# Weights of the convolution's second product: from channel-interleaved to one run of 128 per channel

## The chip, the cores and the metric

One core of a Trainium2 chip runs the whole program. The metric is the device time of one execution in microseconds; a lower time is better. Of the kernel before there are three timed runs and one profiled execution.

## What is computed

The input r has 8 sequences of 2048 steps and 512 channels. The reference normalises it over the channels, convolves each channel with its own long kernel (a state-space model with 64 complex states), applies gelu, normalises, and adds the input; then comes a gated recurrence-like block and a second residual. Cut to what matters here:

```
x = r
K = dplr_kernel(B, C, P, Q, Lam, step, 2048)          # one kernel of 2048 taps for each of 512 channels
h1 = irfft(rfft(layernorm(x)) * rfft(K))[:, :2048]    # causal convolution along the sequence
x = x + layernorm(gelu(h1 + D * layernorm(x), approximate=False))
x = x + layernorm(ffn(layernorm(x)))
```

The kernel computes the causal convolution without a Fourier transform. The sequence is cut into NJ = 16 blocks of P = 128 steps. Within a block a 128x128 matrix made of the first 128 taps is applied; what comes from all earlier blocks is carried by a state x of 128 numbers (64 complex states), which a chain of matrix products moves from block to block. A second product turns the state into output: for each channel a 128x128 matrix, which this text calls the channel's readout weights. All products are made in float16 halves, high and low, so that each product is three matmuls.

## The kernel before, in words

**Stages.** Up to about 150 us the kernel sets up: it reads the input block by block for the layer norm (`stats`, L585 on), builds the powers of the state matrix (`aps`), and runs the state chain for the first two groups of channels. From 158.5 to 656 us it convolves: 512 channels in NG = 16 groups of G = 32. Then the feed-forward part runs until 2899 us; its matmuls are those of L950.

**One group of the convolution** (g = 1 to 14) is a loop of 16 steps. In step s_ the kernel does `conv_mm` for two channels of group g, and between them a link of the chain of group g + 1: `chain_hi` (2 matmuls, L661) and `chain_lo` (1 matmul, L667, and then `split`, which writes the high half with ScalarE, L101, and the low half with VectorE, L102). The low half of a link is an operand of the next `chain_lo`. One `tap_step` and one `chain_in` (3 matmuls) follow. So TensorE has in a step 12 matmuls of `conv_mm`, 6 of the chain and in steps 1 to 12 three of a tap step. Beside it VectorE, ScalarE and GpSimd normalise the input of group g + 2 (`norm_x`: L641 GpSimd, L643 VectorE, L645 ScalarE, L647 GpSimd) and prepare the weights of the feed-forward part (L392 to L409). Group 0 has no chain beside it, and group 15 (`conv_last`) works in two passes, over 4 blocks and then over 12.

**The order.** In the groups the order on TensorE, VectorE, ScalarE and GpSimd is the order in which the program is written (`manual_schedule`), with each engine strictly in its own order. In the setup the order is chosen by a scheduler that plans with estimated durations. DMAs are all issued by SyncE's queue, in order.

**The readout weights** live in a tile `m` for each half group of HS = 16 channels: [128 partitions, 2 halves, 128 columns, 16 channels] before the change. The first 4 of the 128 columns are copied by GpSimd (`load_taps`, L683) from a tile `mb`; `tap_step` doubles the columns: it multiplies columns k to k + kw, for all 16 channels at once, with a power of the state matrix (3 matmuls of kw * 16 = 64, 128, 256 or 512 columns), and `split` writes the product to columns n + k to n + k + kw. There are 6 tap steps for each half group. `conv_mm` (L708) and `conv_last` (L744) then use one channel of `m` as the weights of three matmuls: a load of 128 columns that lie 16 elements apart. The other operand of the convolution, the first 128 taps, is in a tile `t0` (shown as `t`), laid out in the same interleaved manner, and is read by the three matmuls before.

`mm3` (L450 to L452) is the helper that issues three matmuls; the profile gives its lines, and the tile tells which product it is: pyt<-u,t and pyt<-x,m are the two halves of the convolution, pmt<-m,aps is a tap step, pxt<-u,bm is `chain_in`.

Of the kernel before, what the change touches and what calls it, by code (L numbers as in the profile page):

```python
# [10 lines left out]
F16 = mybir.dt.float16  # L11
# [8 lines left out]
P = 128  # L20
L = 2048
H = 512
NB = 8
# [5 lines left out]
HS = 16  # L29
# [30 lines left out]
def s4_gated_block(ctx, tc, a, dbg=None):  # L60
    nc = tc.nc
    V, S, T, Q = nc.vector, nc.scalar, nc.tensor, nc.gpsimd
# [33 lines left out]
    aps = kp.tile([P, LEV + 1, 2, P], F16, name="aps")  # L96
# [3 lines left out]
    def split(hi, lo, src):  # L100
        S.activation(hi, src, AF.Copy)  # L101
        V.tensor_tensor(lo, src, hi, ALU.subtract)  # L102
# [5 lines left out]
    cb = kctx.enter_context(tc.tile_pool(name="cb", bufs=2))  # L108
# [339 lines left out]
    def mm3(out, w, x, start=True, stop=True):  # L448

        T.matmul(out, lhsT=w(0), rhs=x(0), start=start, stop=False)  # L450
        T.matmul(out, lhsT=w(1), rhs=x(0), start=False, stop=False)
        T.matmul(out, lhsT=w(0), rhs=x(1), start=False, stop=stop)  # L452
# [28 lines left out]
    def forms(q, t, i, xa, pt):  # L481

        for h in range(2):
            for k in range(KT):
                T.transpose(pt[h][:, k], xa[h][:, k * P : (k + 1) * P], ident)  # L485
        b1 = FJ.tile([P, 2, 2, P], F32, name="b1", tag="un")
        ts = FJ.tile([P, 4, 2, P], F32, name="ts", tag="ws")
        for h in range(2):
            S.activation(b1[:, h], pt[h][:, 0:2], AF.Copy)
        V.tensor_tensor(ts[:, 0:2], pt[1].rearrange("p (a k) c -> p a k c", a=2), b1, ALU.subtract)  # L490
        V.tensor_tensor(ts[:, 2], pt[1][:, 2:4], ts[:, 0], ALU.subtract)
        V.tensor_tensor(ts[:, 3], ts[:, 2], pt[0][:, 2:4], ALU.subtract)

        def halves():
            if i == 0:
                xfs[q, t] = (FT if t % 2 else FE).tile([P, 7, 2, 2, BP], F16, name="xf")
            xf, cs = xfs[q, t], slice(i * P, (i + 1) * P)
            for f, src in ((slice(0, 3, 2), pt[0].rearrange("p (a k) c -> p a k c", a=2)), (1, pt[1][:, 2:4]), (slice(3, 7), ts)):
                split(xf[:, f, 0, :, cs], xf[:, f, 1, :, cs], src)

        return halves
# [15 lines left out]
    def early_y(sl, y):  # L517

        v = y.rearrange("p (c b) h -> p c b h", b=NB)
        for i in range(2):  # L520
            Q.tensor_copy(early["y"][i][:, :, sl], v[:, i:QC:2, 0:2])
# [58 lines left out]
    with ExitStack() as cctx:  # L580
# [93 lines left out]
        def load_taps(g):  # L674

            for sl in (2 * g, 2 * g + 1):
                t0 = cb.tile([P, 2, P, HS], F16, name="t0", bufs=3)
                base = kpad[:, sl, 1 : P + 1, :]
                tap = bass.AP(base.tensor, base.offset, [[HS, P], [2 * P * H, 2], [1, P * HS]])
                dma(out=t0.rearrange("p i t h -> p i (t h)"), in_=tap)  # L680
                t0s[sl] = t0
                m = cb.tile([P, 2, P, HS], F16, name="m", bufs=4)
                Q.tensor_copy(m[:, :, 0:4, :], mb[:, :, :, sl * HS : (sl + 1) * HS])  # L683
                ms[sl] = m

        def tap_step(sl, lv, k):
            m, n = ms[sl], 1 << lv
            kw = min(n, 512 // HS)
            pmt = pm_.tile([P, 512], F32, name="pmt")
            pv = pmt[:, 0 : kw * HS]  # L690
            mm3(pv, lambda i: aps[:, lv, i, :], lambda i: m[:, i, k : k + kw, :].rearrange("p k h -> p (k h)"))
            split(m[:, 0, n + k : n + k + kw, :].rearrange("p k h -> p (k h)"),
                  m[:, 1, n + k : n + k + kw, :].rearrange("p k h -> p (k h)"), pv)

        def tap_steps(g):
            steps = [(lv, k) for lv in range(2, LEV) for k in range(0, 1 << lv, min(1 << lv, 512 // HS))]
# [2 lines left out]
        def conv_mm(g, hg):  # L699

            u, x = us[g], xs_[g]
            if hg % 4 == 0:
                pys[g] = py.tile([P, 4, NJ * NB], F32, name="pyt")
            sl, hm = 2 * g + hg // HS, hg % HS
            t0, m = t0s[sl], ms[sl]
            o = pys[g][:, hg % 4, :]
            mm3(o, lambda i: t0[:, i, :, hm], lambda i: u[:, :, i, hg, :], stop=False)
            mm3(o[:, NB:], lambda i: m[:, i, :, hm], lambda i: x[:, :, i, hg * NB : (hg + 1) * NB], start=False)  # L708

        def conv_out(g, c4):  # L710

# [15 lines left out]
        def conv_last(g):  # L727

            u, x = us[g], xs_[g]
            yt = {}  # L730
            for j0, j1, hn in ((0, JF, HS), (JF, NJ, 4)):
                n = j1 - j0
                for sl in (2 * g, 2 * g + 1):
                    t0, m = t0s[sl], ms[sl]
                    if j0 == 0:
                        yt[sl] = cb.tile([P, NJ * NB, HS], F32, name="y")
                    y = yt[sl][:, j0 * NB : j1 * NB]
                    for h0 in range(0, HS, hn):
                        pyt = py.tile([P, hn, n * NB], F32, name="pyt")
                        for hm in range(h0, h0 + hn):  # L740
                            hg = sl % 2 * HS + hm
                            o, c = pyt[:, hm - h0], NB if j0 == 0 else 0
                            mm3(o, lambda i: t0[:, i, :, hm], lambda i: u[:, j0:j1, i, hg, :], stop=False)
                            mm3(o[:, c:], lambda i: m[:, i, :, hm],  # L744
                                lambda i: x[:, max(j0 - 1, 0) : j1 - 1, i, hg * NB : (hg + 1) * NB], start=False)
                        S.activation(y[:, :, h0 : h0 + hn], pyt.rearrange("p h c -> p c h"), AF.Gelu, scale=unsc)  # L746
                    if j0 == 0:
                        early_y(sl, yt[sl])
                    dma(out=y_d[j0:j1, :, sl].rearrange("j p b h -> p j (b h)"), in_=y.rearrange("p (j b) h -> p j (b h)", b=NB))
                if j0 == 0:  # L750
                    early_row(0, (1,))

            for i in range(2):
                pt = [pm_.tile([P, KT, P], F32, name="pmt") for _ in range(2)]
                forms(0, 0, i, [normed[i], normed[i + 2]], pt)()
            early_row(1)
            for cj in range(QC):
                dma(out=x1_d[cj, :, 0], in_=early[cj][1][:, 0])

        mb = cm.tile([P, 2, 4, H], F16, name="mb")  # L760
        for k in range(4):
            pmt = pm_.tile([P, 512], F32, name="pmt")
            lv, src = ((0, None), (0, 0), (1, 0), (1, 1))[k]
# [10 lines left out]
        for g in range(2):  # L774
            load_taps(g)
            for st_ in tap_steps(g):
                tap_step(*st_)
# [23 lines left out]
        for g in range(NG):  # L801
# [17 lines left out]
            with tc.manual_schedule(engines=MAN if nxt else MAN | {mybir.EngineType.SP}):  # L819
                if ahead:  # L820
                    load_taps(g + 1)
                    if g == NG - 2:
                        mctx.close()
                    taps = tap_steps(g + 1)
                    chain_in(g + 1, 0)
                if nn:
                    load_x(g + 2)
                if not nxt:
                    early_tiles()
                    for sl in (2 * g - 2, 2 * g - 1):  # L830
                        early_y(sl, ys[sl])
                    dma(out=fcol, in_=a["fcol"])
                    weights(2)
                    early_row(0, (0,))
                    conv_last(g)
                    continue
                norms = [(k - lag, part) for k in range(NJ // JP + 1) for part, lag in ((0, 0), (2, 1), (1, 0), (3, 1))]
                for s_ in range(NJ):
                    if s_ % 2 == 0 and s_:
                        conv_out(g, s_ // 2 - 1)  # L840
                    if nn:

                        d = ND1 if g == 1 else 0
                        while norms and s_ >= d and (s_ == NJ - 1 or len(norms) > 4 + 2 * NJ * (NJ - 1 - s_) // (NJ - d)):
                            norm_x(g + 2, *norms.pop(0))

                    conv_mm(g, 2 * s_)
                    if ahead and s_ < NJ - 1:
                        chain_hi(g + 1, s_)
                    conv_mm(g, 2 * s_ + 1)  # L850
                    if ahead and s_ < NJ - 1:
                        chain_lo(g + 1, s_)
                    if ahead and 1 <= s_ <= 12:
                        tap_step(*taps[s_ - 1])
                    if ahead and s_ < NJ - 2:
                        chain_in(g + 1, s_ + 1)
                    for f in work.get((g, s_), ()):
                        f()
# [395 lines left out]
    with tc.manual_schedule(engines=MAN | {mybir.EngineType.SP}):  # L1254
        before = None
        for n, (q, t) in enumerate(steps):
# [8 lines left out]
            for sl, key in enumerate(zs + gs if n else gs[:5] + zs + gs[5:]):  # L1265
                p = 16 * n + 2 * sl
# [85 lines left out]
```

## Time and profile before

| what | value |
|---|---|
| three timed runs | 2898.7, 2899.93, 2905.06 us; median 2899.93 |
| the profiled execution: its own time, its span | 2900.85 us, 2899.1 us |
| mean granted TensorE clock | 0.962 |
| busy: PE, weight loads, DVE, ACT, POOL | 89%, 78%, 73%, 51%, 41% |
| first and last matmul with weights from `m` | 158.5 and 655.6 us |
| matmuls pyt<-x,m (and as many pyt<-u,t) | 3 x 544 |
| DMA, mean over the span | 156 GB/s |

PE is the row of matmuls and PEld that of weight loads, which overlap matmuls. [...] Windows of a stage show in this order: the stretch, its length, the busy time of PE, PEld, DVE, ACT and POOL with the number of instructions, the granted clock, the share of DMA and its GB/s.

### The profile page before, as it was taken

How to read it: one execution, taken by the hardware profiler on the slowest of the kernel's cores; microseconds unless marked ns; L12 is line 12 of the kernel's file. 1: busy time of each engine (PE TensorE's matmuls, PEld its weight loads, DVE VectorE, ACT ScalarE, POOL GpSimd, SP SyncE). 2: the span in 40 equal slices, each digit the busy share in tenths (PEclk: the TensorE clock that was granted, in tenths of full speed). 3: DMA queues.
4: the chain of work that ended last, by engine and by line, in shares of the span. 5: the costliest groups of instructions: out<-in, count | busy, mean ns of one | idle time of the engine just before them, and what ended most of it. 6: DMA issues, size and time to landing. Idle time of an engine off the chain costs nothing.

```text
span 2899.1 us, 60027 instructions
## 1 busy us (share of the span) xinstructions
PE 2588.2 (89%) x23940; PEld 2255.6 (78%) x23940; DVE 2102.1 (73%) x4248; ACT 1478.8 (51%) x3091; POOL 1185.9 (41%) x1496
## 2 busy tenths in 40 slices
PE   4678888885999999999999998999999899999990
PEld 3367777774888888878888886888888788888870
DVE  7868877747666776667777776777777677777757
ACT  8956666643434443445555454454545445444435
POOL 5757667714112221114454341345443324443227
PEclk8789999987999999999999999999999999999995
DMA  6867878787423433324664443355554334532338
GB/s 233 304 209 241 259 251 260 241 248 189 154 66 95 114 84 96 91 88 124 160 172 135 121 124 99 101 159 167 145 149 120 117 89 147 151 117 89 95 119 298
DMA packets 521937, 451.10 MB, mean 156 GB/s; under 512 B 289974, under 2 KB 401080, under 8 KB 516664
## 3 DMA queue, kind: packets, MB, share of 16 engines
q1 hardware_dynamic: 521224, 446.74, 52.0%
q8 instruction: 187, 3.06, 0.4%
q14 instruction: 94, 0.77, 0.1%
q10 hardware_dynamic: 432, 0.52, 0.1%
HBM read 295.41 MB, written 151.78 MB: 154 GB/s over the span
## 4 chain that ended last, share of the span: by engine, by line
PE 50%; DVE 13%; ACT 5%; DMA 4%; issue 2%; POOL 1%; SPq 0%; POOLq 0%; DVEq 0%; ACTq 0%
PE u L950 47%; PE pt L485 1%; DVE u L992 1%; DMA z_d<-zc 1%; DVE cf L1051 1%; ACT xf L101 1%; DVE cd L1037 1%; DMA y<-y_d 1%; ACT gate L1016 1%; DVE sty L462 1%; DVE gate L1036 1%; ACT y L903 1%; DMA z_d<-zt 1%; DVE u2p L989 1%; DVE sth L462 1%
## 5 line engine op out<-in xcount | busy, mean ns | idle before, releaser
L950 PEld LDWEIGHTS <-w 128*128 128x128 f16 x15120 | 1482.0, 98 | 216.0 <-issue 30.8
L950 PE MATMUL u<-xf,w 128*128 128x256 f16 x8064 | 945.4, 274 | 32.1 <-ACT zt L1003 15.4
L950 PE MATMUL u<-cf,w 128*128 128x256 f16 x7056 | 825.9, 273 | 1.5 <-DVE cf L1051 1.5
L950 PE MATMUL u<-w,xf 128*128 128x256 f16 x2688 | 314.2, 275 | 15.2 <-DVE u L992 5.2
L1141 POOL TENSOR_TENSOR x1r<-x1r,zr 128x512 f32<-128x512 f32 x96 | 133.6, 1392 | 453.8 <-ACT zr L1140 344.6
L988 ACT ACTIVATE u2p<-u 128x256 f32<-128x256 f32 x256 | 96.7, 378 | 433.9 <-PE u L950 433.7
L1016 ACT ACTIVATE gate<-u,bias 128x512 f32<-128x512 f32 (+1 forms) x384 | 200.6, 574 | 217.9 <-PE u L950 217.8
L904 POOL TENSOR_TENSOR xr<-y,xr 128x512 f32<-128x512 f32 x120 | 160.1, 1354 | 351.7 <-ACT y L903 351.5
L950 PEld LDWEIGHTS <-xf 128*128 128x128 f16 x2688 | 264.6, 99 | 49.8 <-issue 10.7
L989 DVE TENSOR_TENSOR u2p<-u2p,u 128x256 f32<-128x256 f32 x256 | 106.8, 417 | 258.7 <-ACT u2p L988 256.8
L992 DVE TENSOR_TENSOR u<-u,u2p 128x512 f32<-128x512 f32 x256 | 179.0, 699 | 8.8
L647 POOL TENSOR_TENSOR u<-xg,u 128x512 f16<-128x512 f32 x104 | 128.7, 1242 | 124.6 <-ACT u L645 124.6
L641 POOL TENSOR_TENSOR xg<-xg,mu 128x512 f32<-128x512 f32 x112 | 162.7, 1459 | 9.7 <-DMA xg<-in_xr 9.7
L471 POOL TENSOR_TENSOR rsy<-rsy,nhalf 128x2 f32<-128x2 f32 (+1 forms) x68 | 49.4, 726 | 284.3 <-DVE rsy L465 272.4
L102 DVE TENSOR_TENSOR x<-pxt,x 128x256 f16<-128x256 f32 x240 | 100.1, 418 | 70.7 <-ACT x L101 69.5
L1021 DVE SCALAR_TENSOR_TENSOR gate<-gate,gate 128x1024 f32<-128x1024 f32 x64 | 88.2, 1378 | 83.2 <-ACT gate L1016 82.8
L462 DVE BATCH_NORM_STATS2 sty<-y 128x6 f32<-128x512 f32 x120 | 76.8, 682 | 86.9 <-DMA y<-y_d 86.9
L1123 POOL TENSOR_TENSOR zr<-zr,ur 128x512 f32<-128x512 f32 x96 | 125.7, 1309 | 20.9 <-DMA zr<-z_d 16.4
L101 ACT ACTIVATE x<-pxt 128x256 f16<-128x256 f32 x240 | 91.2, 381 | 79.6 <-PE pxt L667 73.4
L452 PE MATMUL pyt<-u,t 128*128 128x128 f16 (+2 forms) x544 | 124.8, 229 | 5.5 <-POOL u L623 5.5
L450 PE MATMUL pyt<-u,t 128*128 128x128 f16 (+2 forms) x544 | 121.8, 224 | 6.2 <-ACT y L746 3.1
L101 ACT ACTIVATE xf<-pt 128x512 f16<-128x512 f32 x124 | 60.7, 490 | 128.6 <-DVE xf L102 116.5
(371 smaller groups left out, 5352.2 us busy)
## 6 DMA issues: line engine op xcount, KB each, us to landing
xs<-in_rr SPq DMA_DIRECT2D x32, 1024.0 KB, 7.1
t<-kpad SPq DMA_DIRECT2D x32, 1024.0 KB, 5.5
y_d<-y SPq DMA_DIRECT2D x30, 1024.0 KB, 7.5
xr<-in_r SPq DMA_DIRECT2D x60, 512.0 KB, 5.6
xa<-x_d SPq DMA_DIRECT2D x120, 256.0 KB, 4.1
y<-y_d SPq DMA_DIRECT2D x59, 512.0 KB, 5.8
x_d<-xr SPq DMA_DIRECT2D x59, 512.0 KB, 3.2
xg<-in_xr SPq DMA_DIRECT2D x28, 1024.0 KB, 8.3
```

Source lines behind the costliest of these rows:

```text
L101: S.activation(hi, src, AF.Copy)
L452: T.matmul(out, lhsT=w(0), rhs=x(1), start=False, stop=stop)
L462: V.bn_stats(st[:, i], v)
L641: Q.tensor_tensor(xg, xg, bc(mu1), ALU.subtract)
L647: (V if g == 2 else Q).tensor_tensor(u[:, js, 1], xg, u[:, js, 0], ALU.subtract)
L904: Q.tensor_tensor(xv, yv, xv, ALU.add)
L950: T.matmul(u[:, d], lhsT=w(f, b, i == 1, k), rhs=x(f, b, i == 2, k), start=opens and bank not in seen, stop=stop and j == len(n) - 1, skip ...
L989: V.tensor_tensor(u2, u2, u[:, UY], ALU.add)
L992: V.tensor_tensor(u[:, 2:4], u[:, 2:4], u2[:, None].to_broadcast([P, 2, BP]), ALU.add)
L1016: act = lambda o, s_, b: S.activation(o, s_, AF.Tanh, scale=gsc[kind], bias=b)
L1123: Q.tensor_tensor(s_["z"], s_["z"], us_[c], ALU.add)
L1141: Q.tensor_tensor(s_["x"], s_["x"], s_["z"], ALU.add)
```

## The change

The tile `m` gets the channel as its third axis and the 128 columns as its last, so that a channel's 128 weights of a half lie side by side. The copy of the first 4 columns, the tap step's operand and results, and both readers follow. The products keep their sizes; a tap step's product is now ordered channel by channel (h, then k).

```diff
-                m = cb.tile([P, 2, P, HS], F16, name="m", bufs=4)
-                Q.tensor_copy(m[:, :, 0:4, :], mb[:, :, :, sl * HS : (sl + 1) * HS])
+                m = cb.tile([P, 2, HS, P], F16, name="m", bufs=4)
+                Q.tensor_copy(m[:, :, :, 0:4].rearrange("p i h k -> p i k h"), mb[:, :, :, sl * HS : (sl + 1) * HS])
...
             pv = pmt[:, 0 : kw * HS]
-            mm3(pv, lambda i: aps[:, lv, i, :], lambda i: m[:, i, k : k + kw, :].rearrange("p k h -> p (k h)"))
-            split(m[:, 0, n + k : n + k + kw, :].rearrange("p k h -> p (k h)"),
-                  m[:, 1, n + k : n + k + kw, :].rearrange("p k h -> p (k h)"), pv)
+            pv = pv.rearrange("p (h k) -> p h k", h=HS)
+            mm3(pv, lambda i: aps[:, lv, i, :], lambda i: m[:, i, :, k : k + kw])
+            split(m[:, 0, :, n + k : n + k + kw], m[:, 1, :, n + k : n + k + kw], pv)
...
-            mm3(o[:, NB:], lambda i: m[:, i, :, hm], lambda i: x[:, :, i, hg * NB : (hg + 1) * NB], start=False)
+            mm3(o[:, NB:], lambda i: m[:, i, hm, :], lambda i: x[:, :, i, hg * NB : (hg + 1) * NB], start=False)
...
-                            mm3(o[:, c:], lambda i: m[:, i, :, hm],
+                            mm3(o[:, c:], lambda i: m[:, i, hm, :],
                                 lambda i: x[:, max(j0 - 1, 0) : j1 - 1, i, hg * NB : (hg + 1) * NB], start=False)
```

In the lists of instructions of the two built kernels the groups 1 to 15 have the same order on every engine, with other shapes for the tap steps. In the setup the order differs on PE, DVE, ACT, POOL and SyncE: tap steps, links of the chain and statistics are interleaved differently.

## Prediction

> **What bounds the kernel now.** I read the windows of the convolution first, then the weight loads by tile, then starts in the timeline of TensorE, then the waits of one group. The weights of `m` are used from 158.5 to 655.6 us only, so the feed-forward part (2200 us) keeps its work; the change can only move its start.
>
> First, durations (min/median/max) of weight loads of line 450: `m` is read with a step of 16 elements, `bm` in one run.
>
> ```profile
> L450 PEld LDWEIGHTS <-m x544: 143/149/174, 158.5 to 655.4; 128*128 128x128 f16 x182
> L450 PEld LDWEIGHTS <-bm x240: 95/98/151, 102.6 to 624.6; 128*128 128x128 f16 x120
> ```
>
> A load overlaps a matmul, so a duration is no pace. The pace is in the starts. A tap step of 64 columns, whose weights `aps` lie in one run, and the first pass of the last group, with 24 columns and weights of `m`:
>
> ```profile
> 308.00 0.19 PE L450 MATMUL pmt<-m,aps 128*128 128x64 f16 x1
> 308.03 0.19 PE L451 MATMUL pmt<-m,aps 128*128 128x64 f16 x1
> 308.05 0.19 PE L452 MATMUL pmt<-m,aps 128*128 128x64 f16 x1
> 308.08 0.27 PE L450 MATMUL pxt<-u,bm 128*128 128x256 f16 x1
> ...
> 635.12 0.22 PE L450 MATMUL pyt<-x,m 128*128 128x24 f16 x1
> 635.18 0.22 PE L451 MATMUL pyt<-x,m 128*128 128x24 f16 x1
> 635.24 0.21 PE L452 MATMUL pyt<-x,m 128*128 128x24 f16 x1
> 635.30 0.22 PE L450 MATMUL pyt<-u,t 128*128 128x32 f16 x1
> ```
>
> 64 columns go at 28 ns each; 24 columns with interleaved weights need 62 ns. So an interleaved load costs about 62 ns of pace, whatever the matmul, and a load in one run at most 28. The ordinary matmul of `m` has 120 columns; tap steps of 128 and 256 columns start 55 and 109 ns apart, 0.42 ns a column and 2 ns, so 120 columns need 52.5 ns. In the groups they start 59 to 63 ns apart: they are bound by their loads, by a small margin.
>
> Does TensorE set the pace of a group? A group repeats every 31.8 us (the eighth gelu of each group). One such stretch and one window:
>
> ```profile
> 250.00:300.00 50.00, 43.67 (x493) 37.43 (x492) 40.39 (x72) 33.73 (x74) 33.48 (x28) 1.00 0.81 249
> ...
> PE pxt L667 <- DVE x L102: 4.1, 4, 1.3
> DVE x L102 <- ACT x L101: 3.9, 8, 0.8
> DVE xg L643 <- POOL xg L641: 0.8, 1, 0.8
> ```
>
> Only in part: four times a group TensorE waits about 1 us for the low half of the state, because VectorE has long work in front of it. From 307 us:
>
> ```profile
> 306.74 0.77 DVE L643 TENSOR_TENSOR xg<-xg,rs 128x512 f32<-128x512 f32 x1
> 307.42 0.41 DVE L102 TENSOR_TENSOR x<-pxt,x 128x256 f16<-128x256 f32 x1
> 308.67 1.76 DVE L643 TENSOR_TENSOR xg<-xg,rs 128x512 f32<-128x512 f32 x1 [0.83 <-POOL xg L641]
> 310.36 0.41 DVE L102 TENSOR_TENSOR x<-pxt,x 128x256 f16<-128x256 f32 x1
> ...
> 306.20 0.75 POOL L683 COPY m<-mb 128x128 f16<-128x128 f16 x1
> 306.92 2.97 POOL L641 TENSOR_TENSOR xg<-xg,mu 128x512 f32<-128x512 f32 x2
> ```
>
> The reader sees a chain in which TensorE has no part: GpSimd's copy for `m`, its L641, VectorE's L643, the low half at 310.36, `chain_lo` at 310.82. Between such a wait and the last event before it that TensorE set, a faster TensorE only waits longer.
>
> **Part by part.**
>
> *Readout matmuls in the groups.* For a channel the three starts after a matmul of `m` are 59, 63 and 63 ns apart; with loads that fit under the stream they become 52.5: 6.5 + 10.5 + 10.5 = 27.5 ns, 28 with rounding. 32 channels: 0.90 us a group. What of it stays? Going through the period from 290.6 to 322.4 us: `chain_lo` at 295.48 follows an unbroken run of VectorE from the tap product that TensorE started at 290.62; the stretch from 299.66 to 315.28 is four such runs in a row. TensorE paces only 295.5 to 299.7 and 315.3 to 322.4, with 4 + 8 = 12 channels: 12 x 28 = 0.34 us. Within these the low half is ready 0.4 to 0.5 us before it is needed, so 58 ns a step uncover nothing. Groups 1 to 13: 13 x 0.34 = 4.4 us. Bounds: 0, and 13 x 0.9 = 11.7 if all stays.
>
> *Group 0 and the end.* Group 0 has TensorE without chain: 62.7 ns a matmul at full clock, 376 ns a channel, which become about 346; 20 of 32 channels run at full clock: 0.6 us. In group 14 DMA is near its limit (0.94 from 600 to 610 us). In the last group's first pass 32 x 3 gaps of 62 ns could fall to about 28: 3.3 us, but the gelu behind it waits 11.4 us for a DMA of y. Together I take 1 us, bounds 0 and 3.6.
>
> *GpSimd's copy* stands in the chain shown above, 128 elements, 0.28 us alone and 0.75 beside VectorE. It now writes with a step of 256 bytes. No row shows such a copy. Nearest: L618 writes with a step of 32 bytes at 683 ns for 256 elements, L623 in one run at 685, so nothing; the dearest elementwise row, L641, has 2.85 ns an element, 0.36 us for 128, so at most +0.15 with its start-up. I take 0.05, nearer to L618: 13 x 0.05 = +0.6 us, bounds 0 and 2. [...]
>
> *Tap steps.* 12 a group; operand and results now go in pieces of 4 to 32 elements, 256 bytes apart. TensorE: the matmuls of u move pieces of 8 elements and after a 256-column matmul start 55 ns apart with 128 columns, so pieces cost nothing. ScalarE: L717 reads and writes scattered pieces of 4 elements at 689 ns for 512, L1016 in one run at 681. I take nothing. VectorE's low half (686 ns for 512) has no such row; lower bound 0, upper bound as a rival.
>
> *Setup.* The work is the same, its order is not. Before, GpSimd does eight L641 for group 2 ahead of the last low half of block 15 (L623), and the last four wait for a DMA: L623 ends at 159.1, and TensorE stood still from 152.7 to 158.5. In the new list two pairs move from ahead of the last statistics (L612) to behind them, and four stand behind L623. From the last figures of block 15 (141.7) I add, in the new order, L610, L613, two L618, L614, two L623, L611 and L612: 5.2 us, so L612 ends near 147 instead of 151.4; four L641 (4.9 us) and one L623 give 152.5. But TensorE now has five `chain_lo` between the second and third matmul of the convolution, a loop of 0.31 + 0.42 + 0.47 = 1.2 us each, behind VectorE's second L643, which ends near 151.5: 151.97 + 3 x 1.19 = 155.5 for the last. The start of the convolution moves from 158.5 to about 155.5: 3 us. Bounds: 148.2, where nothing but statistics is in the way (10 us), and 3 us later than before, if the state's input comes later (four more tap products stand ahead of it on TensorE, 0.4 to 0.6 us each on ScalarE).
>
> *Clock.* The standstill costs the clock:
>
> ```profile
> 152.00:158.00 6.00, 0.37 (x2) 0.23 (x2) 0.14 (x1) 2.01 (x3) 5.08 (x5) 0.50 0.24 88
> 158.00:160.00 2.00, 1.48 (x15) 1.47 (x15) 0.00 (x0) 0.00 (x0) 1.11 (x2) 0.50 0.00 0
> 164.00:168.00 4.00, 4.00 (x67) 4.00 (x66) 3.42 (x6) 3.13 (x6) 0.56 (x1) 1.00 0.30 72
> ```
>
> 12 channels took 0.62 us instead of 0.376: 2.9 us. With links of the chain up to the start the clock may stay at 1.00, as it did at such a density from 130 to 149 us. I take half, 1.5; bounds 0 and 2.9.
>
> **Sum:** -4.4 - 0.6 - 1 + 0.6 - 3 - 1.5 = -9.9 us against the profiled execution's own 2900.85 (span 2899.1): 2891.0. The median of the timed runs is 0.9 lower; the range covers that.
>
> **Rivals.**
>
> 1. The setup gives nothing. For it: its order follows estimates, and four tap products move ahead of the state's input. Against it: the L641 leave GpSimd's way. -4.4 - 0.6 - 1 + 0.6 = -5.4: 2895.5.
> 2. The loads of `m` do not get faster in the new layout. -3 - 1.5 + 0.6 = -3.9: 2897. Against it: `bm` and `aps`, 98 ns and a pace of 28. [...]
> 3. All of the readout's gain stays, because VectorE's runs move together with TensorE: -11.7 in place of -4.4, 2883.7. For it: all engines wait for one another; against it, the unbroken runs.
> 4. Slower: VectorE's and ScalarE's tap results in short pieces. Place: the 512-column products at 292.1 and 301.1 us begin two of the runs that end in a wait; each has one ScalarE and one VectorE pass on the path, four passes a group. It takes 15.7 us, 1.2 a group, to turn my sum into a loss over 0.2%: 0.3 us a pass (0.69 to 1.0). At twice the time, +0.64 us a pass, it is 13 x 2.6 = 33 us: 2924. For it: no row of such a write on VectorE; against it: L717.
>
> **Chances.** Forecast 0.49 (its own range 2886 to 2894), setup gives nothing 0.19, loads unchanged 0.08, all stays 0.11, slower 0.13. A measurement can tell about 0.2%, 5.8 us, from no change. Faster: 0.49 + 0.11 = 0.60; within: 0.27; slower: 0.13. The range from 2881 to 2900 takes in all but the last and some of the setup's worst bound.
>
> **What would show it.** Weight loads of `m` at 98 ns; starts of pyt<-x,m 52 to 53 ns apart; a period of 31.45 us in groups 2 to 13, with waits at `chain_lo` longer by some 0.1 us each; third matmul of the convolution near 155.5; the copy under 0.8; tap passes at 0.69 and 0.60. Wrong would be: a period unchanged, tap passes over 0.8, or a convolution that starts after 158.5.

## The result, and the profile after

The changed kernel takes 2882.49 us (median of 6 runs, 2880.8 to 2887.53) where the kernel before takes 2898.3 (6 runs, 2894.93 to 2905.06): a ratio of 0.9945, 95% interval 0.9932 to 0.9959, or 15.8 us less. In a later comparison it was 2885.39 against 2899.79 us (6 and 25 runs), ratio 0.9947, 0.9935 to 0.9959, or 14.4 us less. The forecast was 9.9 us less. The profiled execution took 2880.99 us, its span 2879.2, at a mean granted clock of 0.963: 19.9 us below the profiled execution of before.

Weight loads of `m` by line (minimum/median/maximum in ns); the line shown of before had 143/149/174:

```profile
L450 PEld LDWEIGHTS <-m x544: 95/105/152, 152.8 to 640.8; 128*128 128x128 f16 x182
L451 PEld LDWEIGHTS <-m x544: 95/98/153, 152.8 to 640.8; 128*128 128x128 f16 x182
```

The pace is in TensorE's timeline (start in us, duration), again in the first pass of the last group:

```profile
619.81 0.18 PE L450 MATMUL pyt<-x,m 128*128 128x24 f16 x1
619.84 0.18 PE L451 MATMUL pyt<-x,m 128*128 128x24 f16 x1
619.87 0.18 PE L452 MATMUL pyt<-x,m 128*128 128x24 f16 x1
619.89 0.23 PE L450 MATMUL pyt<-u,t 128*128 128x32 f16 x1
619.96 0.22 PE L451 MATMUL pyt<-u,t 128*128 128x32 f16 x1
```

With weights of `m` the starts are now about 25 ns apart and no longer 62; with weights of `t`, which stayed interleaved, they are still 60 to 70. In the groups, matmuls of 120 columns start 52 to 53 ns apart, as forecast.

A stretch of 50 us among the groups (length, then PE, PEld, DVE, ACT, POOL busy, granted clock, DMA share) and the waits of TensorE and VectorE in it:

```profile
240.00:290.00 50.00, 42.86 (x499) 36.48 (x497) 40.96 (x72) 33.93 (x75) 34.84 (x28) 1.00 0.83 251
...
PE pxt L667 <- DVE x L102: 6.7, 6, 1.4
DVE xg L643 <- POOL xg L641: 0.8, 1, 0.8
```

The same line over 50 us of before, from 250 to 300:

```profile
PE pxt L667 <- DVE x L102: 6.1, 6, 1.3
```

TensorE has less work and waits more for the low half. Over one period the four long waits of TensorE add up to 4.1 us before and 4.5 us now. A group repeats every 31.52 us instead of 31.80. The chain that the prediction showed, one period of the changed kernel:

```profile
296.66 0.76 DVE L643 TENSOR_TENSOR xg<-xg,rs 128x512 f32<-128x512 f32 x1
297.34 0.41 DVE L102 TENSOR_TENSOR x<-pxt,x 128x256 f16<-128x256 f32 x1
298.59 1.75 DVE L643 TENSOR_TENSOR xg<-xg,rs 128x512 f32<-128x512 f32 x1 [0.84 <-POOL xg L641]
300.26 0.41 DVE L102 TENSOR_TENSOR x<-pxt,x 128x256 f16<-128x256 f32 x1
...
296.12 1.26 POOL L683 COPY m<-mb 128x128 f16<-128x128 f16 x1
296.95 2.84 POOL L641 TENSOR_TENSOR xg<-xg,mu 128x512 f32<-128x512 f32 x2
```

The copy's record is 0.51 us longer (1.26 for 0.75), but L641 begins 0.83 us behind the copy's start where it was 0.72, and from the copy's start to the low half at the end of the chain it is 4.14 us (296.12 to 300.26) where it was 4.16 (306.20 to 310.36). The chain has the same length: L641 starts 0.11 us later behind the copy, but the two L641 take 2.84 us together where they took 2.97.

The largest part lies at the start of the convolution:

```profile
152.00:158.00 6.00, 5.89 (x94) 5.70 (x92) 3.37 (x5) 5.16 (x9) 6.00 (x7) 1.00 0.14 46
158.00:160.00 2.00, 2.00 (x38) 2.00 (x36) 2.00 (x2) 0.61 (x3) 2.00 (x2) 1.00 0.17 29
```

TensorE was busy 0.37 us of the six from 152 to 158; now it is 5.89, and the granted clock is 1.00 where it was 0.50.

Where the time went, in us from the span's start (third matmul of the convolution, the first that needs the low half of the input, then the eighth gelu of groups 1, 12 and 15, then the rest of the span), for eight kernels whose orders in the setup are either that of before or that of the changed kernel. Each row is one profiled execution:

| kernel | layout, setup's order | third matmul | group 1 | group 12 | group 15 | rest |
|---|---|---|---|---|---|---|
| before | old, old | 158.52 | 212.68 | 562.45 | 652.91 | 2246.2 |
| after | new, new | 152.77 | 203.42 | 550.19 | 638.64 | 2240.6 |
| after, again | new, new | 152.14 | 203.98 | 550.85 | 639.92 | 2246.1 |
| late | new from group 2, old | 159.07 | 214.10 | 560.84 | 650.52 | 2245.7 |
| order_only | old, new | 151.48 | 204.34 | 555.73 | 645.73 | 2247.6 |
| copy_runs | new, old | 159.22 | 214.21 | 562.41 | 650.85 | 2249.3 |
| warm | old, old | 159.10 | 212.05 | 561.88 | 651.81 | 2242.2 |
| copy_more | old, old | 157.91 | 211.31 | 564.30 | 655.24 | 2245.0 |

### The profile page after: what moved, and what is told of

It reads as the page before. It is cut to its first block, busy times and chain, and to the rows that moved or that the text cites. A ratio compares the mean times of both kernels' runs of the same rounds, so it can differ in the third digit from the quotient of the medians.

```text
span 2879.2 us, 60023 instructions
## 1 busy us (share of the span) xinstructions
PE 2568.3 (89%) x23940; PEld 2235.5 (78%) x23940; DVE 2103.6 (73%) x4248; ACT 1478.1 (51%) x3091; POOL 1198.5 (42%) x1496
## 4 chain that ended last, share of the span: by engine, by line
PE 52%; DVE 12%; ACT 4%; DMA 4%; issue 2%; POOL 1%; SPq 0%; POOLq 0%; DVEq 0%; ACTq 0%
PE u L950 49%; PE pt L485 1%; DVE u L992 1%; DVE cf L1051 1%; ACT xf L101 1%; DVE cd L1037 1%; ACT gate L1016 1%; DMA z_d<-zc 1%; DVE gate L1036 1%; DVE sty L462 1%; DVE u2p L989 1%; ACT y L903 1%; DMA z_d<-zt 1%; DMA y<-y_d 1%; DVE xf L102 1%
## 5 line engine op out<-in xcount | busy, mean ns | idle before, releaser
L647 POOL TENSOR_TENSOR u<-xg,u 128x512 f16<-128x512 f32 x104 | 128.8, 1242 | 114.0 <-ACT u L645 113.9
L641 POOL TENSOR_TENSOR xg<-xg,mu 128x512 f32<-128x512 f32 x112 | 162.7, 1459 | 6.2 <-DMA xg<-in_xr 6.2
L102 DVE TENSOR_TENSOR x<-pxt,x 128x256 f16<-128x256 f32 x240 | 99.9, 418 | 63.3 <-ACT x L101 62.7
L667 PE MATMUL pxt<-x,at 128*128 128x256 f16 x224 | 61.9, 276 | 73.1 <-DVE x L102 72.0
L450 PE MATMUL pyt<-u,t 128*128 128x128 f16 (+2 forms) x544 | 121.5, 223 | 6.1 <-ACT y L746 6.1
```

Of the source, the lines that this page charges most:

```text
L641: Q.tensor_tensor(xg, xg, bc(mu1), ALU.subtract)
L647: (V if g == 2 else Q).tensor_tensor(u[:, js, 1], xg, u[:, js, 0], ALU.subtract)
```

## The experiments

All times are medians, beside runs of the kernel before on the same chip (2900.89 us, 31 runs, for the first four; 2901.94, 21 runs, for the next four; 2899.79, 25 runs, for the last four). The kernels dup and steps24 have one run each and are compared by their traces.

**late: the layout without the order.** The new layout in groups 2 to 15, the old lines for the first four half groups.

```diff
+                if sl >= 4:
                     m = cb.tile([P, 2, HS, P], F16, name="m", bufs=4)
...
+                else:
+                    m = cb.tile([P, 2, P, HS], F16, name="m", bufs=4)
...
```

> New layout of m in groups 2 to 15 only; groups 0 and 1, and with them the order of the setup on every engine, as before the change. Theory: the gain has two independent parts, the readout matmuls (period 31.80 to 31.52 us, and the end) and the order of the setup (start, clock, groups 0 and 1). Here only the first is there: third matmul of the convolution near 158.5, eighth gelu of group 1 near 212.7 as before, period 31.52 in groups 3 to 12, time -5 us against before (-3.5 to -6.5). Rival: the readouts give most of the gain, -10 us or more; then the eighth gelu of group 15 must be 10 us earlier without an earlier start.

2894.97 us, 5.9 less; ratio 0.9981, 0.9972 to 0.9990. Start 159.07, period 31.52. So the layout from group 2 on gives about 6 us by the medians (2.9 to 8.1 by the interval); the rival, 10 us or more, is out. The profiled executions show 3.8 us of it in place: from the eighth gelu of group 1 to that of group 15 it is 436.4 us where it was 440.2. The other 2 us are not located.

**order_only: the order without the layout.** Only the loop order of the copy is turned, which changes no byte of the result, yet gives the new order on every engine. That the scheduler has another estimate for a copy in this form is the likely reason; the runs show only that the form of the copy decides the order.

```diff
-                Q.tensor_copy(m[:, :, 0:4, :], mb[:, :, :, sl * HS : (sl + 1) * HS])
+                Q.tensor_copy(m[:, :, 0:4, :].rearrange("p i k h -> p i h k"), mb[:, :, :, sl * HS : (sl + 1) * HS].rearrange("p i k h -> p i h k"))
```

> Old layout of m throughout, only the loop order of the copy for m is turned (channel outside, column inside), which gives the setup the same order on every engine as the changed kernel has. Theory: third matmul of the convolution near 152.8, granted clock 1.00 from there, eighth gelu of group 1 near 204, period still 31.80, loads of m still 149 ns; time -9 to -10 us. Rival (the order is worth no more than the 3 to 6 us of the earlier start): -6 or less. If the copy takes as long as in the changed kernel (1.05 us mean) and its length counts, the period is longer than 31.80 and the time only -3.

2893.61 us, 7.3 less; ratio 0.9978, 0.9964 to 0.9991. Start 151.48, group 1 8.3 us earlier, and the loads of `m` are still slow (means of 151 to 154 ns). It was expected 9 to 10; the period is 31.94 and not 31.80, 1.6 us over 11 groups. By the medians the order (7.3 us, interval 2.6 to 10.4) and the layout (5.9, 2.9 to 8.1) cannot be told apart; in the traces the order gives 8.3 us up to group 1, before that loss, and the layout 3.8 us from there on. So the order, which the edit was not about, is worth about as much as the layout or more.

**copy_runs: the layout everywhere, in the old order.** The copy with the column as inner loop; with it the setup's plan falls back to the old order.

```diff
-                Q.tensor_copy(m[:, :, :, 0:4].rearrange("p i h k -> p i k h"), mb[:, :, :, sl * HS : (sl + 1) * HS])
+                Q.tensor_copy(m[:, :, :, 0:4], mb[:, :, :, sl * HS : (sl + 1) * HS].rearrange("p i k h -> p i h k"))
```

> New layout of m throughout, the copy for m with the column as inner loop, so that it writes runs of 4 elements; the order of the setup is that of before. Theory: start near 158.5, period 31.52, time -5.5 us against before (the readout part, group 0 included), whatever the copy takes. Rival (the copy's extra half microsecond counts in each group): if the copy is back near 0.5 us here, the period falls below 31.52, towards 31.1, and the time is -10 or better in spite of the old start; if it is longer than 1.05 us, the period is longer than 31.52.

2897.06 us, 3.8 less; ratio 0.9990, 0.9981 to 0.9999. Start 159.22. The copy is shorter by its record (mean 631 ns instead of 1046), and the period is 31.66, longer than the changed kernel's 31.52: neither expectation. So the recorded length of the copy does not set the period: in order_only it has a mean of 1.04 us, as in the changed kernel, and yet order_only loses what this kernel loses. Both kernels with the turned loop lose 0.13 to 0.15 us a group against the kernel with the same layout, all of it before the first wait for the low half. In both, the L643 of that stretch takes 0.88 to 0.89 us instead of 0.76 to 0.77; from order_only:

```profile
330.66 0.89 DVE L643 TENSOR_TENSOR xg<-xg,rs 128x512 f32<-128x512 f32 x1
331.48 0.41 DVE L102 TENSOR_TENSOR x<-pxt,x 128x256 f16<-128x256 f32 x1
...
330.12 1.25 POOL L683 COPY m<-mb 128x128 f16<-128x128 f16 x1
330.97 2.95 POOL L641 TENSOR_TENSOR xg<-xg,mu 128x512 f32<-128x512 f32 x2
```

What the two copies have in common, and the other two not, is that they read `mb` with a step of 1 KB from element to element. Why L643 beside them takes 0.12 us more was not tested.

**warm: the clock alone.** The kernel before, with 15 matmuls of 512 columns into an unused accumulator during the standstill.

```diff
+            if g == 0 and hg == 0:
+                w = py.tile([P, 512], F32, name="pyt")
+                idle = lambda n: [T.matmul(w, lhsT=aps[:, 2, 0, :], rhs=ch16[:, 0, :], start=True, stop=True) for _ in range(n)]
...
+                T.matmul(o, lhsT=t0[:, 1, :, hm], rhs=u[:, :, 0, hg, :], start=False, stop=False)
+                idle(15)
+                T.matmul(o, lhsT=t0[:, 0, :, hm], rhs=u[:, :, 1, hg, :], start=False, stop=False)
...
```

> The kernel before with 15 extra matmuls of 512 columns into an unused accumulator between the second and the third matmul of the convolution, where TensorE stands still for 5.5 us; nothing else moves in the setup. Theory that the low clock costs time by itself: the third matmul stays at 158.5 and the first 12 channels take 0.37 us instead of 0.62, eighth gelu of group 0 up to 3 us earlier, time -1 to -3 us. Rival (group 0 is then held by the normalisation beside it, or by its start alone): eighth gelu of group 1 unchanged within 0.5 us and time within 1 us of before.

2898.5 us, 2.4 less; ratio 0.9991, 0.9983 to 1.0000: hardly to be told by the time. The trace tells more. These matmuls (L709) fill the standstill, at a granted clock of 0.57, and the clock is at 1.00 when the third matmul starts:

```profile
153.72 5.09 PE L709 MATMUL pyt<-ch,aps 128*128 128x512 f16 x15
159.10 0.22 PE L713 MATMUL pyt<-u,t 128*128 128x128 f16 x1 [0.30 <-POOL u L623]
...
154.00:156.00 2.00, 2.00 (x7) 0.73 (x6) 0.00 (x0) 1.15 (x1) 2.00 (x3) 0.57 0.20 72
158.00:159.00 1.00, 0.80 (x4) 0.33 (x3) 0.00 (x0) 0.00 (x0) 1.00 (x2) 1.00 0.00 0
160.00:162.00 2.00, 2.00 (x36) 2.00 (x34) 0.09 (x1) 1.21 (x2) 0.00 (x0) 1.00 0.51 131
```

From the third matmul, 12 channels take 4.35 us (before 5.81, late 6.23); to the eighth gelu of group 1 it is 52.95 us, against 54.16, 55.03, 54.99 and 53.40 in the four kernels with the old order and the low clock (mean 54.4). To the eighth gelu of group 0 it is 12.17 us, against 13.30 to 14.06. So the clock by itself is worth about 1.5 us, 1.1 to 1.9 by group 0; the rival, nothing, is out.

**dup: where TensorE's time counts.** The changed kernel with extra readouts, in even groups in steps that end in a wait, in odd groups in steps 5 to 8.

```diff
-            mm3(o[:, NB:], lambda i: m[:, i, hm, :], ..., start=False)
+            twice = 2 <= g <= 13 and hg // 2 in ((2, 4, 10, 14), (5, 6, 7, 8))[g % 2]
+            for last in (False, True) if twice else (True,):
+                mm3(o[:, NB:], lambda i: m[:, i, hm, :], ..., start=False, stop=last)
```

> The changed kernel, in groups 2 to 13 with the readout of four steps done twice (8 channels, 24 matmuls of 52 ns, 1.26 us of TensorE more a group; the readout of these channels is counted twice in the output): steps 2, 4, 10 and 14 in even groups, which end in a wait of TensorE for the low half, and steps 5 to 8 in odd groups, which by the prediction's reading are paced by TensorE. Theory (TensorE's time counts only where no wait follows before VectorE's runs): even groups keep 31.5 us (at most +0.15), odd groups become 0.9 to 1.26 us longer, 32.4 to 32.8. Rival (all of TensorE's time counts, the waits move along): both +1.26. Rival (the group is held by the other engines altogether): neither moves.

Groups 2, 4, 6, 8, 10 and 12 take 31.50 to 31.56 us, groups 3, 5, 7, 9 and 11 take 32.47 to 32.50. The same 1.26 us of TensorE costs nothing in one place and 0.96 in the other. Both rivals are out, and the reading behind "12 of 32 channels" holds where it was tried: for the four steps that end in a wait, and for 8 of the 12 channels, with three quarters of their time.

**steps24: layouts in between.** A channel's weights 2 elements apart in even half groups and 4 in odd ones.

```diff
-                m = cb.tile([P, 2, HS, P], F16, name="m", bufs=4)
+                c = (2, 4)[sl % 2]
+                m = cb.tile([P, 2, HS // c, P, c], F16, name="m", bufs=4)
...
```

> Layouts between the two: the weights of a channel lie 2 elements apart in the even half groups and 4 apart in the odd ones (16 before, 1 after the change). Theory that the load's cost depends on the step: at 4 elements (8 bytes) something between 98 and 149 ns, at 2 elements nearer to 98; starts after a matmul of m between 52 and 63 ns. Rival that only one run is fast: both at 149 ns and 59 to 63 ns. Rival that any step up to a limit is fast: both at 98 ns and 52 ns.

| step of the weights | median load, groups 3 to 11 | start to start, 120 columns | 24 columns |
|---|---|---|---|
| 1 element (after) | 98 ns | 52 | 25 |
| 2 (4 bytes) | 98 | 52 | 25 |
| 4 (8 bytes) | 113 | 52 | 30 to 33 |
| 16 (before) | 150 | 61 | 62 |

The first theory holds at the four steps that were run: nothing at 2, 5 to 8 ns of pace at 4, 37 at 16. The step of 4 in an odd half group, three starts at 24 columns:

```profile
621.20 0.19 PE L450 MATMUL pyt<-x,m 128*128 128x24 f16 x1
621.23 0.18 PE L451 MATMUL pyt<-x,m 128*128 128x24 f16 x1
621.26 0.18 PE L452 MATMUL pyt<-x,m 128*128 128x24 f16 x1
621.29 0.22 PE L450 MATMUL pyt<-u,t 128*128 128x32 f16 x1
```

For a stream of 120 columns a step of 4 paces like one run (52 ns). The kernel itself repeats a group every 31.70 us, longer than the changed kernel's 31.52; it also makes the copy for `m` in two instructions, and which of the two differences costs this was not tested.

**copy_more: is GpSimd in the chain?** The kernel before with one more copy behind the copy for `m`, from group 2.

```diff
                 Q.tensor_copy(m[:, :, 0:4, :], mb[:, :, :, sl * HS : (sl + 1) * HS])
+                if sl >= 4:
+                    mz = cb.tile([P, 2, HS, 4], F16, name="mz", bufs=2)
+                    Q.tensor_copy(mz.rearrange("p i h k -> p i k h"), mb[:, :, :, sl * HS : (sl + 1) * HS])
```

> The kernel before with a second copy of the same kind right behind the copy for m in groups 2 to 15, written in the order of the changed kernel into a tile that nothing reads; no other order changes. If GpSimd's time at this place counts, L641 begins 0.75 to 0.85 us later and the period of groups 2 to 12 becomes 32.5 to 32.65: +10 us. Rival (there is slack, or GpSimd makes it up beside VectorE): 31.80 to 31.95, at most +2 us.

2903.44 us, 1.5 more; ratio 1.0008, 1.0000 to 1.0017; period 32.09. That is 0.29 us a group, between the two expectations, and all of it appears ahead of the second wait for the low half, as the chain says. So GpSimd's time counts there, but less than half of it (the copy's record has a mean of 0.71 us). The trace shows where the rest goes:

```profile
305.72 0.76 POOL L683 COPY m<-mb 128x128 f16<-128x128 f16 x1
306.42 0.94 POOL L686 COPY mz<-mb 128x128 f16<-128x128 f16 x1
307.17 2.52 POOL L641 TENSOR_TENSOR xg<-xg,mu 128x512 f32<-128x512 f32 x2
```

L641 starts 1.45 us behind the first copy instead of 0.72, but the two L641 then take 2.52 us instead of 2.97.

**copy_S, cS_lo0, cQ_s1, cQ_s2: the copy out of the chain.** Four versions of the changed kernel: both copies of a group on ScalarE; one of them on ScalarE in an idle stretch; or that one on GpSimd one or two steps later.

```diff
-                Q.tensor_copy(m[:, :, :, 0:4].rearrange("p i h k -> p i k h"), ...)
+                (S.copy if sl >= 4 else Q.tensor_copy)(m[:, :, :, 0:4].rearrange("p i h k -> p i k h"), ...)
```

> The changed kernel with the copy for m on ScalarE instead of GpSimd in groups 2 to 15, everything else in the same order. If the copy stands in a chain that ends in TensorE's second wait of a group (copy, two L641, second L643, low half), L641 begins 0.7 us earlier, the wait before the second L643 (0.84 us) goes, and the period falls to 30.8: -9 us against the changed kernel, about -25 against before. Rival: L641 then runs beside the first L643 and both get longer (L643 takes 0.77 us beside the copy and 1.75 beside L641), so the low half before it is up to 0.9 us later and the period stays within 0.15 of 31.52 or grows.

In the others, the copy of the odd half group became a function of its own, called in the loop of steps:

```diff
+                    if ahead and s_ == 1:                          # cQ_s1; s_ == 2 in cQ_s2
+                        copy_taps(2 * g + 3, Q.tensor_copy)
...
                         chain_lo(g + 1, s_)
+                        if s_ == 0:                                # cS_lo0
+                            copy_taps(2 * g + 3, S.copy)
```

> The changed kernel with the copy of the odd half group on ScalarE, but emitted behind the first high half of the new chain, where ScalarE is idle for 1.4 us, so that nothing urgent stands behind its wait for the buffer; the even half group's copy stays on GpSimd. A copy more on GpSimd cost 0.29 us a group, and the copy on ScalarE shortened the stretch from the first to the second wait from 2.92 to 1.78 us. Theory (the copy is a link of that chain, and only the place on ScalarE was wrong): first wait unmoved, period 30.4 to 31.2, 4 to 14 us below the changed kernel. Rival (VectorE beside L641 gets slower by as much): 31.4 to 31.6, no gain.

> The changed kernel with the copy of the odd half group still on GpSimd, but between the two L641 instead of ahead of them; nothing else moves. Theory: the first L641 begins up to 0.8 us earlier, the second L643 with it, period 31.1 to 31.4, 1 to 5 us below the changed kernel. Rival: the tap step that needs the copy comes late, or the second L641 is as urgent as the first: 31.5 to 31.8.

> The same copy one step later, behind both L641 and the next low half on GpSimd. Theory: the chain is free of it as on ScalarE, 30.6 to 31.3, if the tap step of that half group does not wait. Rival: TensorE waits for the copy at the first tap step of the odd half group, and with it the chain of the next group: 31.8 or more.

| kernel | time, and ratio to before | period | first to second wait | L641's waits for DMA, whole run |
|---|---|---|---|---|
| after, again | 2885.39; 0.9947 (0.9935 to 0.9959) | 31.53 | 2.92 us | 6.7 us |
| copy_S | 2906.38; 1.0015 (1.0005 to 1.0025) | 33.1 | 1.78 | 51.2 |
| cS_lo0 | 2905.45; 1.0017 (1.0007 to 1.0028) | 33.1 | 1.75 | 51.4 |
| cQ_s1 | 2895.61; 0.9984 (0.9974 to 0.9993) | 32.4 | 1.76 | 47.3 |
| cQ_s2 | 2907.39; 1.0022 (1.0013 to 1.0031) | 33.3 | 1.91 | 45.3 |

All four are slower than the changed kernel. The stretch in which the copy stood became 1.0 to 1.2 us shorter, as the theory has it; but the last wait of a group, from the start of the matmul before it, grew from 1.43 us to 2.5 to 2.8, and the stretch from it to the first wait grew from 3.16 us to 4.0 to 4.9. "Nothing else moves" was wrong: on TensorE, VectorE and SyncE's queue the order is unchanged, but on GpSimd, without the copy in its place, an L641 came forward, ahead of L647s that had stood before it. The text on the kernel says that the order in the groups is the written one. For GpSimd the traces show otherwise: `load_taps` writes its two copies one behind the other, and in the trace of before they start at 290.13 and 306.20 us. What sets GpSimd's order stays open. The input of that L641 is still being loaded, and all that GpSimd has behind it waits. GpSimd and VectorE in cQ_s1:

```profile
324.01 1.28 POOL L641 TENSOR_TENSOR xg<-xg,mu 128x512 f32<-128x512 f32 x1 [3.44 <-DMA xg<-in_xr]
325.25 2.13 POOL L647 TENSOR_TENSOR u<-xg,u 128x512 f16<-128x512 f32 x1
327.35 1.73 POOL L641 TENSOR_TENSOR xg<-xg,mu 128x512 f32<-128x512 f32 x1
...
326.30 1.64 DVE L643 TENSOR_TENSOR xg<-xg,rs 128x512 f32<-128x512 f32 x1
327.86 0.41 DVE L102 TENSOR_TENSOR x<-pxt,x 128x256 f16<-128x256 f32 x1
```

The same two engines in the changed kernel, at the same place of a group:

```profile
322.81 1.28 POOL L641 TENSOR_TENSOR xg<-xg,mu 128x512 f32<-128x512 f32 x1
326.52 1.16 POOL L647 TENSOR_TENSOR u<-xg,u 128x512 f16<-128x512 f32 x1 [2.42 <-ACT u L645]
327.62 1.25 POOL L683 COPY m<-mb 128x128 f16<-128x128 f16 x1
...
325.10 0.68 DVE L643 TENSOR_TENSOR xg<-xg,rs 128x512 f32<-128x512 f32 x1
325.70 0.41 DVE L102 TENSOR_TENSOR x<-pxt,x 128x256 f16<-128x256 f32 x1
```

In the one, GpSimd's late work (here L647, then L641) runs beside VectorE, whose L643 takes 1.64 us, and the low half behind it is late; in the other, GpSimd is idle and L643 takes 0.68. What makes L643 longer there, the lines do not show. Whether the copy's move would gain with L641 held in its place was not tried. None of the four beats the changed kernel.

**after_again.**

> The changed kernel itself, on one chip with the three others, so that they have something to be compared with. Eighth gelu of group 15 near 638.6 (638 to 640.5), period 31.52, time 13 to 18 us below before. Of the 19.9 us between the two profiled executions, 5.6 lay behind the convolution, where no instruction was changed; in the other executions that part took 2242 to 2249 us without regard to the layout. If it is spread, it lies in that range here; if the change causes it, it is again near 2240.

2885.39 us, 14.4 less. Group 15 at 639.92, period 31.53, and the rest of the span is 2246.1 us, where the first profile had 2240.6 and before 2246.2. So the 5.6 us behind the convolution are spread between executions and not the change; the table shows 2240.6 to 2249.3 without regard to the layout.

## Why the prediction was right in sign and too small

The sum by its own steps, in us:

| step | predicted | measured |
|---|---|---|
| readout in groups 2 to 12, a group | -0.34 | -0.28 together with the copy |
| copy, a group | +0.05 (0 to 0.15) | nothing on the chain; its record +0.5 |
| group 13 and the end (group 12 to 15) | -1.3 | -2.0 and -1.4 (90.46 to 88.45 and 89.07) |
| start of the convolution | -3 (-10 to +3) | -5.8 and -6.4 |
| clock | -1.5 (-2.9 to 0) | -1.5 (warm) |
| groups 0 and 1, besides the clock | -0.9 | -1.0 to -2.2 (from 52.86 to 51.84 and 50.65) |
| tap passes | 0 | 0 |
| behind the convolution | 0 | spread |

- *Readout.* Right in mechanism. The loads went to 98 ns, the starts to 52, and the period fell by 0.28 us; net of the copy the forecast was 0.29. That this is so close is partly luck: the readout gave 0.06 less than its 0.34, and the copy cost nothing instead of 0.05 (the period of 31.45 that the prediction named as a sign leaves the copy out). The rival in which all 0.90 stays is out, though its 2883.7 us lies nearer to the measured time than the forecast's 2891.0: the period would have been 30.9. And dup shows why: ahead of a wait, time of TensorE only changed the wait (31.50 to 31.56 us a group with 1.26 us more of it, against 31.52). The stretch from 315.28 us to the next such wait, in which the prediction put 8 of its 12 channels (0.22 us), went from 12.00 to 11.81 us. The stretch with its other 4 channels (0.11 us) went from 9.24 only to 9.20.
- *Loads not faster.* Out: 98 ns, as `bm` had (105 on line 450). For the same 128 columns the runs show 98, 98, 113 and 150 ns at steps of 1, 2, 4 and 16 elements.
- *Copy.* The forecast left its record out of bounds: 0.50 more on the mean (510 to 1046 ns), where the upper bound was 0.15, and its sign "the copy under 0.8" failed. The price on the path, which the sum used, was nothing. The start of the next instruction moved by 0.11 us, not 0.5. The upper bound was the author's estimate: 128 elements at L641's 2.85 ns, and a start-up that no row shows. The 0.28 us that the prediction calls alone were not alone: at 290.13 us VectorE was in an L102 (290.06 to 290.75); the 0.75 at 306.20 stood beside its L446 and L643.
- *Setup.* That the setup gives nothing is out by order_only. This is the term that was mis-sized: -3 for -5.8 to -6.4. Up to group 15 the two profiled executions gained 4.4 and 3.1 us more than the forecast; the start is 2.8 and 3.4 of that. For GpSimd the time came right by luck: four L641 and one L623 were to end at 152.5, and the first low half of the two L623 ends near 152.7. But L612 ended at 145.8 and not 147, and the four L641 took 6.3 us and not 4.9. What failed is the sentence that five links of the chain take "1.2 us each" behind VectorE's second L643, "151.97 + 3 x 1.19 = 155.5 for the last". Two groups' chains run alternately, so one group's loop passes while the other's link runs:

```profile
151.35 0.27 PE L667 MATMUL pxt<-x,at 128*128 128x256 f16 x1 [0.86 <-DVE x L102]
...
152.00 0.27 PE L667 MATMUL pxt<-x,at 128*128 128x256 f16 x1
152.11 0.27 PE L450 MATMUL pxt<-u,bm 128*128 128x256 f16 x1
152.22 0.27 PE L451 MATMUL pxt<-u,bm 128*128 128x256 f16 x1
152.33 0.27 PE L452 MATMUL pxt<-u,bm 128*128 128x256 f16 x1
152.44 0.38 PE L661 MATMUL pxt<-x,at 128*128 128x256 f16 x2
152.66 0.27 PE L667 MATMUL pxt<-x,at 128*128 128x256 f16 x1
152.77 0.22 PE L452 MATMUL pyt<-u,t 128*128 128x128 f16 x1
```

The first link behind VectorE's second L643 is at 151.35, not 151.97, and only two follow, not three. They are 0.65 us apart, the time of TensorE's own six matmuls, and the last is at 152.66, where 155.5 was reckoned. The trace of before already had this distance between its last two links:

```profile
148.64 0.27 PE L667 MATMUL pxt<-x,at 128*128 128x256 f16 x1 [0.78 <-DVE x L102]
...
149.29 0.27 PE L667 MATMUL pxt<-x,at 128*128 128x256 f16 x1
```

GpSimd delivered the low half of the input at the same time as the last link:

```profile
144.16 1.67 POOL L612 TENSOR_TENSOR rs<-ve,nhalf 128x8 f32<-128x8 f32 x1
145.79 6.29 POOL L641 TENSOR_TENSOR xg<-xg,mu 128x512 f32<-128x512 f32 x4
152.05 1.29 POOL L623 TENSOR_TENSOR u<-xc,u 128x256 f16<-128x256 f32 x2
```

- *Clock.* The size is right by two errors. "12 channels took 0.62 us" was wrong: in the trace of before only the first six did, the others 0.37 to 0.38, and by windows the granted clock is 0.50 to 162 us and 0.91 from there to 163. So the bound was 6 x 0.245 = 1.5 us and not 2.9. Of the doubled bound half was taken, for fear that the clock would not stay up; it stayed at 1.00, and about the whole 1.5 came: the 12 channels took 4.37 us where they had taken 5.81, and in this difference the readout's gain (about 0.3) and a new pause of TensorE (0.3, at 152.87, until the last low half of the state is written) nearly cancel.
- *Groups 0 and 1.* In group 0 a channel takes 0.35 us where at full clock it took 0.37: 32 x 0.02 = 0.6, as forecast. Group 1 also holds a wait of ScalarE for a store of `y`: 2.0 us before and 2.2 to 3.5 in late, copy_runs, warm and copy_more, but 0.8 in order_only, 0.6 in after_again and none in the first profile of the changed kernel. How much of the rest is this wait and how much the readout is not settled.
- *Short pieces on VectorE and ScalarE*, the rival on the other side. Out: the tap passes of 512 columns have means of 686 and 595 ns (before 686 and 596), those of 64 columns 211 and 219 (212 and 218).

With 11 periods the terms of the measured column add up to between 12.8 and 15.2 us. The eighth gelu of group 15 came 13.0 and 14.3 us earlier in the two profiled executions, and the medians differ by 14.4 and 15.8; the 19.9 between the first two profiled executions holds 5.6 of spread.

## What to carry to other kernels

Lay weights so that a load reads them in one run or with a step of 4 bytes (98 ns a load here, against 113 at 8 bytes and 150 at 32), but count the saving only where no wait follows before another engine's run; an extra matmul placed in different steps tells where that is (1.26 us of it cost nothing in some steps and 0.96 us in others). Where a scheduler plans with estimates, an edit of one small copy can move the whole list, and here that was worth about as much as the edit's own purpose or more (8.3 us up to group 1, against 3.8 from there on): compare the lists of both kernels and reckon the critical stretch of each. When chains of two groups alternate, a loop's time may count once for the pair and not for every link: here links stood 0.65 us apart where 1.19 was reckoned.

## What the runs showed of the hardware that was not expected

- A load took 98, 98, 113 and 150 ns at steps of 1, 2, 4 and 16 elements of two bytes, at a pace of 25, 25, 30 to 33 and 62 ns for 24 columns. A moving operand in pieces of 4 elements cost at most 2 ns a matmul: tap steps of 64 columns start 30 ns apart (297.91, 297.94, 297.97 in the changed kernel), and 28 ns apart before.
- The copy on GpSimd, 128 elements, had a longer record where it wrote them one by one with a step: on the mean 0.51 us in long runs (before), 0.71 with a step of 8 bytes (the second copy of copy_more), 1.04 with 32 bytes (order_only, which also reads with a step) and 1.05 with 256 bytes (after). In the last case the instruction behind it starts only 0.11 us later. With runs of four elements written and a read step of 1 KB, the record is only 0.12 us longer (510 to 631 ns), yet VectorE's L643 beside it takes 0.12 us more.
- L643 took 0.68 us with GpSimd idle (325.10 us, changed kernel), 1.76 beside L641 and L647 (308.67, before) and 1.64 beside L647 and the next L641 (326.30, cQ_s1); it took 0.77 where L641 began 0.18 us behind it (306.74, before). So a change of order on GpSimd was not free for VectorE here: in four kernels with such a change a group got 0.9 to 1.7 us longer, and the traces show longer L643 and waits for a DMA in it; how much each of the two costs was not separated.
